# Cross-attention on one core: query banks as two tiles, the context's sums in steps, seeds moved, another order in the first rounds and the tail

## The chip, the core and the metric

The kernel runs on one core of a Trainium2 chip. A core has four compute engines that take their instructions each in its own order and wait for each other by semaphores: TensorE (PE, matrix products, with the loading of weights shown as PEld), VectorE (DVE), ScalarE (ACT) and GpSimd (POOL). SyncE (SP) issues the transfers between DRAM and the on-chip memory; SPq in a profile is its queue. Products land in PSUM, which the kernel uses in banks of 128 partitions x 512 float32. The metric is the time of one execution on the device, in microseconds. Two timed runs of the kernel before gave 1520.61 and 1522.45, a median of 1521.53.

## What is computed

For each of 64 batches, `H_l` is a 256 x 512 block of x and `H_a` a 256 x 384 block of the context, all float32:

```python
text_p = jnp.einsum('bld,dh->blh', H_l, W_text) + b_text
audio_p = jnp.einsum('bsd,dh->bsh', H_a, W_audio) + b_audio
Q = layer_norm(text_p, g1, beta1)
K = layer_norm(audio_p, g2, beta2)
V = audio_p
scores = jnp.einsum('blh,bsh->bls', Q, K) * scale
alpha = jax.nn.softmax(scores, axis=-1)
H_hyper = jnp.einsum('bls,bsh->blh', alpha, V)
H_hyper = jnp.einsum('blh,hk->blk', H_hyper, W_out) + b_out
return layer_norm(H_hyper + H_l, g_out, beta_out)
```

## The kernel before

All engines' instructions stand in an order written out by hand: each call in the main function emits instructions, and the engine takes them in the order of the calls. A program then adds the waits that the data need; it tracks them by tile.

**Two projections by fewer products.** The keys (`Thirds`, name k) and the output (`Thirds`, name y, called `o`) are computed in 15 products of 128 x 128 by 128 x 172 instead of 18, the queries (`Fork`) in 7 products of two halves each instead of 8, with sums formed beforehand and afterwards. Each product is two passes of PE and so two rows of a profile. `third_sides` (L298) has GpSimd form seven sums of the transposed context `cT` (tile csum) or of the transposed result `zT` of the attention (tile zsum); the products that need them are numbered. Product 14 and 13, the first two, need the fourth and fifth of these seven operations. `sum_x` (L282) has GpSimd form four sums of the transposed x (tile xsum).

**Stages of a projection.** `Thirds` keeps its partial results in the banks ps_m, ps_l, ps_u, ps_n, the same four for k and o, which take turns. `seed` (L504, ACT) writes a bias into ps_m; `one` writes ps_n, `two` adds to ps_m, `three` to ps_u, and so on to `five`; `after_one`, `after_three`, `after_four` (DVE) carry sums from bank to bank in between. `after_five` (L541, ACT and DVE), `leave` (ACT) and `last_middle` (L552, POOL operations d and kr) take k's result out of the banks; `leave_plus` (L558, DVE) takes o's out and adds x. It calls `between()` in its midst, which is DVE's reciprocal of the softmax sums (`reciprocals`, L682).

`Fork` has one PSUM tile ps_f of two banks (L66): R and q1 in the first, q2 and q3 in the second. `seed` (L583, ACT) writes the bias into R and zeros into q2, in one copy from a prepared tile fork_seed. `one` adds x's first quarter into R, `after_one` (L598, ACT) copies R to q1, `seven` adds into q2, `after_seven` (L601, ACT) copies q2 to s7, `six` adds into R, `after_six` (L608, DVE) writes q3 and steps R, `five` adds into R, `after_five` (DVE) writes q2, and `rest` finishes. `square`, `scales` (POOL: ve and rstd) and `normalise` (ACT) then make the rows of unit variance.

**A round** (L1045 to L1192) works on several batches at once: it projects keys and queries of batch b + 2 (k2, q2), transposes the inputs of b + 3 and forms their sums, turns the stored q and k of b + 1 (through DRAM and back: `store`, `fetch`, `turn` on DVE), takes scores and softmax of b (`at`), the attention's product of b - 1 (`last`, context_one) and b - 2 (`old`, context_two) and the output of `old`, and normalises the output of b - 3 (`settled`: `sums`, `deviations` on ACT with ve and rstd on POOL, `shift` L882 and `settle` L891 on DVE). PE's order in a round is k2.one, k2.two, context_two, k2.three, q2.seven, q2.six, k2.four, q2.five, k2.five, q2.rest, score, o.one, o.two, score, o.three, score, o.four, score, o.five, the next q's one, context_one. Softmax is `maxima` (DVE, nmx), `exponentials` (ACT, e), `reciprocals` (DVE, rden), `divide_e` (ACT); e is stored to DRAM, fetched and turned by DVE (`store_e`, `fetch_e`, `turn_e`, tile eT) for the next round's context_one.

In the steady rounds k2.seed stands behind divide_e (L1189), Fork.seed behind o.five (L1159), and sum_x and third_sides of b + 3 stand together near the round's end, x first (L1165 and L1166). Before the rounds (L925 to L1043) the first batches are projected, the weights of the output folded, and the weights' sums formed (`third_weights`, L324). After them (L1194 to L1293) the last batches are finished; there `transpose_e` (PE) and `copy_e` (ACT) take the place of the way through DRAM for the last two.

Of the kernel before, what the change touches and what calls it, by code (L numbers as in the profile page):

```python
# [22 lines left out]
def kernel(  # L23
# [41 lines left out]
    third = [p_all.tile([P, H], F32, tag=f"t{n}", name=f"ps_{n}") for n in "mlun"]  # L65
    fork = p_all.tile([P, 2, H], F32, tag="fork", name="ps_f")  # L66

# [109 lines left out]
    def keep_busy(n):  # L177

        for _ in range(n):
            nc.tensor.matmul(fork[:, 1, :P], lhsT=ones, rhs=ones, start=True, stop=True)  # L180

# [115 lines left out]

    def third_sides(T, tag, pool=work):  # L298

        a0, a1 = T[:, :, :P], T[:, :, P:]  # L300
        s = pool.tile([P, 10, P], F32, tag=tag, name=tag)
        plus = lambda o, i0, i1: nc.gpsimd.tensor_tensor(o, i0, i1, ALU.add)  # L302
        less = lambda o, i0, i1: nc.gpsimd.tensor_tensor(o, i0, i1, ALU.subtract)  # L303
        less(s[:, 0:2], a0[:, 0:1].broadcast_to([P, 2, P]), a0[:, 1:3])
        less(s[:, 2:4], s[:, 0:2], a1[:, 0:1].broadcast_to([P, 2, P]))
        plus(s[:, 4:6], s[:, 2:4], a1[:, 1:3])
        plus(s[:, 6], s[:, 4], a1[:, 2])
        plus(s[:, 7], s[:, 5], a1[:, 1])
        less(s[:, 8], s[:, 6], a0[:, 2])
        less(s[:, 9], a1[:, 0], a0[:, 0])  # L310
        return {
            14: s[:, 6], 13: s[:, 7], 11: s[:, 0], 12: s[:, 1], 9: s[:, 8], 8: s[:, 2],
            10: s[:, 3], 0: a0[:, 1], 3: a0[:, 2], 1: s[:, 9], 7: a1[:, 0], 2: a1[:, 1],
            4: a1[:, 2], 6: s[:, 4], 5: s[:, 5],
        }

# [55 lines left out]
    class Projection:  # L372
# [79 lines left out]
        def turn(self, halves=range(2)):  # L452
            if 0 in halves:
                self.T = work.tile(
                    [P, HC, self.nt * P], F32, tag=f"{self.name}T", name=f"{self.name}T_{self.b}"
                )
            if self.name == "q" or self.b >= B - 2:
                if 0 in halves:
                    turn(self.T, self.sq, HC)
                return  # L460

            for t in halves:
                nc.vector.transpose(
                    self.T.rearrange("p k (q t j) -> p t q k j", t=self.nt, j=SQ)[:, t],
                    self.sq[:, t * NQ : (t + 1) * NQ].rearrange("p q (k i) -> p q k i", k=HC),
                )
# [14 lines left out]
    class Thirds(Projection):  # L481
# [11 lines left out]
        def add_products(self, *pairs):  # L493
            for n, place in pairs:
                nc.tensor.matmul(  # L495
                    place,
                    lhsT=self.sides[n],
                    rhs=self.weights[n],
                    start=(n == 14),
                    stop=True,  # L500
                    skip_group_check=True,
                )
# [55 lines left out]
        def leave_plus(self, x, between):  # L558
            rows = self.rows
            u, n, v = self.room("u"), self.room("n", 2), self.room("d")  # L560
            dve(n, self.M, ends(x[:, 1]), ALU.add)
            dve(u, self.U, middle(x[:, 1]), ALU.add)
            dve(v, self.N0, u, ALU.add)
            dve(middle(rows[:, 1]), v, self.N1, ALU.subtract)
            dve(ends(rows[:, 1]), self.N, n, ALU.add)
            between()
            u = self.room("u")
            dve(u, self.U, middle(x[:, 0]), ALU.add)
            dve(middle(rows[:, 0]), self.T, u, ALU.add)
            dve(ends(rows[:, 0]), self.L, ends(x[:, 0]), ALU.add)  # L570

    class Fork(Projection):

        R, q1 = fork[:, 0, :H2], fork[:, 0, H2:]
        q2, q3 = fork[:, 1, :H2], fork[:, 1, H2:]

# [5 lines left out]
        @staticmethod  # L582
        def seed():  # L583
            nc.scalar.copy(fork[:, :, :H2], fork_seed)

# [37 lines left out]
        def square(self):  # L623
            self.var = small.tile([P, 2], F32, tag="varq", name="var")
            for t in range(2):
                junk = work.tile([P, H], F32, tag="junk", name="junk")
                nc.scalar.activation(  # L627
                    junk,
                    fork[:, t, :],
                    AF.Square,  # L630
                    scale=1.0 / math.sqrt(H),
                    accum_out=self.var[:, t : t + 1],
                )

        def normalise(self):
            for t in range(2):
                nc.scalar.mul(self.rows[:, t, :], fork[:, t, :], self.r[t])

    class Attention:
# [110 lines left out]
        def start_products(self):  # L750

            sides = third_sides(self.zT, "zsum", once)
            self.o = Thirds("y", self.b, sides, wao_blocks, bao_sb, bao_delta)
            self.y = self.o.rows
# [167 lines left out]
    q, k, xT, cT, xs, cs, att = {}, {}, {}, {}, {}, {}, {}  # L922
    bank = third + [fork[:, n, :] for n in range(2)]

# [49 lines left out]
    k[1].evict(1)  # L974
    fork_seed = const.tile([P, 2, H2], F32, tag="fork_seed", name="fork_seed")
    nc.vector.tensor_copy(fork_seed[:, 0], bt_sb[:, H2:])
    nc.vector.memset(fork_seed[:, 1], 0.0)
    bt_step = const.tile([P, H2], F32, tag="bt_step", name="bt_step")
# [30 lines left out]
    q[1].after_seven()  # L1009
    part = bias_parts()  # L1010
    fold_multiply(2, 0, 2)
    q[1].six()
# [8 lines left out]
    q[1].rest()  # L1021
    wa_t = const.tile([P, 11, W3], F32, tag="wa_thirds", name="wa_thirds")
    wa_blocks = third_weights(wa_sb, wa_t, [0])
    cT[2] = turn_c(2)
    cs[2] = third_sides(cT.pop(2), "csum")
    xT[2] = turn_x(2)
    third_weights(wa_sb, wa_t, [1], nc.vector)
    q[1].square()
    q[1].scales()
    xs[2] = sum_x(xT.pop(2))  # L1030
    ba_delta = third_bias(ba_sb, "ba_delta")
    bao_delta = third_bias(bao_sb, "bao_delta")
    q[1].normalise()
# [11 lines left out]
    for b in range(B - 2):  # L1045
# [18 lines left out]
        if b == 0:  # L1064
            at.score(0, 8)
            Fork.seed()
        k2 = k[b + 2] = Thirds("k", b + 2, cs.pop(b + 2), wa_blocks, ba_sb, ba_delta)
        if b == 0:
# [30 lines left out]
        if settled:  # L1099
            settled.deviations()  # L1100
        k2.four()
        k2.after_four()
# [11 lines left out]
        k2.leave()  # L1114
        k2.last_middle()
        if old:
            old.o.seed()
# [26 lines left out]
        if b:  # L1144
            at.score(4, 7)
        q2.normalise()
        q2.store()
# [15 lines left out]
        k2.fetch()  # L1163
        if three:
            xs[b + 3] = sum_x(xT.pop(b + 3))  # L1165
            cs[b + 3] = third_sides(cT.pop(b + 3), "csum")  # L1166
        if b < 2:
            wao_blocks = third_weights(wao_sb, wao_t, [b])
        at.maxima()
        at.exponentials()  # L1170
        if not three:
            att[b + 1] = Attention(b + 1)
            att[b + 1].affine_queries()
            att[b + 1].affine_keys()
        if last:
# [9 lines left out]
        if last:  # L1185
            last.context_one()
        at.divide_e()
        if three and old:
            k2.seed()  # L1189
        at.store_e()  # L1190
        if last:
# [3 lines left out]
    at = att[B - 2]  # L1195
    last.fetch_e()

    load_x_rows(B - 3)
# [4 lines left out]
    old.o.seed()  # L1203
    at.score(0, 8)
    settled.statistics()
    settled.shift(0)
    settled.shift(1)
    k[B - 1].turn()
    at.maxima()
    at.exponentials()  # L1210
    at.reciprocals()
    old.o.one()
    old.o.after_one()
    old.o.two()
    last.turn_e()
    last.context_one()
# [5 lines left out]
    last.copy_two()  # L1222
    q[B - 1].turn()
    k[B - 1].affine(g2_sb, be2_sb)
    at.transpose_e(bank[4])
    at.copy_e()
    old.o.four()
    old.o.after_four()
    settled.settle(0)
    settled.settle(1)  # L1230
    settled.store()
    last.start_products()
    q[B - 1].affine(g1_sb, be1_sb)
    end = Attention(B - 1)
    old.o.five()
    old.o.leave_plus(x_rows[B - 4], lambda: None)
# [4 lines left out]
    add_bias(B - 1)  # L1241
    end.score(0, 8)
    old.shift(0)
    old.shift(1)
    last.o.one()
    last.o.after_one()
    last.o.two()
    end.maxima()
    end.exponentials()
    end.reciprocals()  # L1250
    at.start_output()
    at.multiply(0, bank[5])
    last.o.three()
    last.o.after_three()
    at.multiply(1, bank[4])
    old.settle(0)
    old.settle(1)
    old.store()
    at.evict(0)
    at.scales(0, 1)  # L1260
    last.o.four()
    last.o.after_four()
    end.transpose_e(bank[5])
    end.copy_e()
    last.o.five()
    at.evict(1)
    at.scale_soon(1)
    last.o.leave_plus(x_rows[B - 3], lambda: None)
    end.context()
    last.statistics()  # L1270
    at.shift(0)
    at.settle(0)
    at.shift(1)
# [52 lines left out]
```

## Time and profile before

| | |
|---|---|
| median of two runs | 1521.53 us |
| the profiled execution | 1522.37 us |
| its span, first to last instruction | 1520.6 us |
| PE busy | 1414.6 us (93%), 7419 matmuls |
| DVE busy | 1184.7 us (78%) |
| ACT busy | 1116.4 us (73%) |
| POOL busy | 983.4 us (65%) |
| moved by DMA | 322.54 MB, 212 GB/s on average |
| mean granted clock of PE | 0.990 |

Durations are those of one execution. An engine's share of busy time is an average over the span; where an engine waits, the profile names who released it last. The start of the next instruction can lie before the recorded end of the one ahead, since both are pipelined: for a chain, distances of starts are added up, not durations. By stretches, PE was busy 21.53 of the 30 us from 30 to 60, 18.84 from 60 to 90 and 25.12 from 90 to 120, at clocks of 0.94, 0.83 and 0.94; 287.08 of the 300 from 1000 to 1300; and 49.45 of the last 71, from 1450 on.

### The profile page before, as it was taken

To read this page: it belongs to the slowest core of one execution; us is meant where nothing else is said; L and a number is where in the kernel's file an instruction comes from. 1 tells how busy PE (TensorE), PEld (TensorE's weight loads), DVE (VectorE), ACT (ScalarE), POOL (GpSimd) and SP (SyncE) were. 2 spreads that over 40 slices of the span, in tenths; PEclk is the share of its full clock that TensorE was granted. 3 is DMA by queue.
4 is the path that set the end of the run, shared out by engine and by line. 5 is a ranking of instruction groups with operands and counts; after the bars stand their busy time and mean duration, and the time that the engine had idled before them with its cause. 6 is when DMAs were issued, how large, how long until landed. Compare 5 with 4: busy or idle time off the path is not lost.

```text
span 1520.6 us, 26267 instructions
## 1 busy us (share of the span) xinstructions
PE 1414.6 (93%) x7419; PEld 1235.6 (81%) x7419; DVE 1184.7 (78%) x2501; ACT 1116.4 (73%) x2813; POOL 983.4 (65%) x1685
## 2 busy tenths in 40 slices
PE   9679999999999999999999999999999999999976
PEld 4468888888888888888888888888888888888864
DVE  6537788788887887887878878878888888787757
ACT  4447877777777777787787787787777777777753
POOL 4576666666666667667667666666666666666724
PEclk9989999999999999999999999999999999999999
DMA  9577889889999889889998988988998988998761
GB/s 214 123 186 192 208 221 235 212 215 238 211 224 232 215 220 230 219 213 227 228 212 220 234 209 220 236 212 212 241 209 222 235 213 220 232 217 212 209 187 70
DMA packets 450456, 322.54 MB, mean 212 GB/s; under 512 B 154885, under 2 KB 382981, under 8 KB 450310
## 3 DMA queue, kind: packets, MB, share of 16 engines
q1 hardware_dynamic: 450214, 320.72, 86.5%
q8 instruction: 60, 0.98, 0.3%
q14 instruction: 86, 0.70, 0.2%
q10 hardware_dynamic: 96, 0.13, 0.0%
HBM read 203.83 MB, written 116.92 MB: 211 GB/s over the span
## 4 chain that ended last, share of the span: by engine, by line
PE 50%; DVE 16%; ACT 12%; DMA 10%; issue 6%; SPq 5%; POOL 2%; DVEq 0%; ACTq 0%; POOLq 0%
PE ps_f L588 15%; PE ps_m L495 11%; PE ps_sc L657 8%; DMA xq<-in_x_dram 7%; PE ps_z L723 4%; PE ps_u L495 4%; SPq L72 4%; PE ps_n L495 4%; ACT e L688 4%; DVE yr L479 3%; ACT kT L470 3%; PE ps_l L495 2%; DVE nmx L667 2%; DVE n L479 2%; DMA ed<-e 1%
## 5 line engine op out<-in xcount | busy, mean ns | idle before, releaser
L657 PE MATMUL ps_sc<-kT,qT 128*128 128x256 f32 x1024 | 261.0, 379 | 2.8 <-ACT zT L738 2.8
L588 PE MATMUL ps_f<-wtsum,xsum 128*128 128x256 f32 x756 | 201.4, 389 | 41.2 <-ACT s L603 39.0
L657 PEld LDWEIGHTS ps_sc<-kT,qT 128*128 128x128 f32 x1024 | 186.4, 190 | 20.5 <-ACT zT L738 3.4
L588 PEld LDWEIGHTS ps_f<-wtsum,xsum 128*128 128x128 f32 x756 | 132.9, 190 | 79.2 <-ACT s L603 64.7
L723 PE MATMUL ps_z<-eT,c 128*128 128x256 f32 x768 | 189.8, 385 | 6.4 <-DVE eT L75 6.4
L303 POOL TENSOR_TENSOR zsum<-zT 128x256 f32<-128x256 f32 x124 | 73.7, 595 | 186.5 <-ACT zT L741 173.9
L723 PEld LDWEIGHTS ps_z<-eT,c 128*128 128x128 f32 x768 | 143.0, 193 | 26.6 <-DVE eT L75 7.3
L674 ACT ACTIVATE e<-ps_sc,nmx 128x256 f32<-128x256 f32 x128 | 59.5, 470 | 130.7 <-DVE nmx L667 130.7
L369 POOL TENSOR_TENSOR rstd<-ve,nhalf 128x2 f32<-128x2 f32 x192 | 136.1, 709 | 16.0
L470 ACT ACTIVATE kT<-kT,columns 128x256 f32<-128x256 f32 x256 | 139.6, 596 | 0.0
L470 ACT ACTIVATE qT<-qT,columns 128x256 f32<-128x256 f32 x256 | 138.7, 591 | 0.0
L479 DVE TENSOR_TENSOR ps_f<-ps_f,s 128x256 f32<-128x256 f32 x126 | 54.5, 432 | 107.1 <-PE ps_f L588 104.1
L588 PE MATMUL ps_f<-wt,xT 128*128 128x256 f32 x504 | 130.5, 382 | 0.0
L367 POOL TENSOR_SCALAR ve<-var 128x2 f32<-128x2 f32 x126 | 27.7, 220 | 142.8 <-ACT junk L627 129.9
L891 DVE SCALAR_TENSOR_TENSOR yr<-yr,rstd,beo 128x512 f32<-128x512 f32 x124 | 114.6, 926 | 0.9 <-POOL rstd L369 0.9
L688 ACT ACTIVATE e<-e,rden 128x256 f32<-128x256 f32 x124 | 56.2, 500 | 71.9 <-DVE rden L684 71.9
L302 POOL TENSOR_TENSOR zsum<-zsum,zT 128x256 f32<-128x256 f32 x186 | 99.9, 552 | 9.7
L302 POOL TENSOR_TENSOR csum<-csum,cT 128x256 f32<-128x256 f32 x186 | 99.1, 547 | 9.7
L303 POOL TENSOR_TENSOR csum<-cT 128x256 f32<-128x256 f32 x124 | 99.4, 801 | 6.9 <-DVE cT L75 6.9
L588 PEld LDWEIGHTS ps_f<-wt,xT 128*128 128x128 f32 x504 | 94.0, 192 | 10.3 <-issue 0.3
L532 DVE COPY t<-ps_u 128x172 f32<-128x172 f32 x124 | 41.8, 337 | 75.6 <-PE ps_u L495 75.6
L882 DVE SCALAR_TENSOR_TENSOR yr<-yr,nm,go 128x512 f32<-128x512 f32 x124 | 93.8, 758 | 7.3 <-ACT junk L775 7.3
(230 smaller groups left out, 3980.1 us busy)
## 6 DMA issues: line engine op xcount, KB each, us to landing
kd<-kr SPq DMA_DIRECT2D x64, 512.0 KB, 4.2
kq<-kd SPq DMA_DIRECT2D x256, 128.0 KB, 3.6
qd<-qr SPq DMA_DIRECT2D x64, 512.0 KB, 4.8
qq<-qd SPq DMA_DIRECT2D x256, 128.0 KB, 3.6
xq<-in_x_dram SPq DMA_DIRECT2D x252, 128.0 KB, 5.5
x<-in_x_dram SPq DMA_DIRECT2D x63, 512.0 KB, 4.3
out_dram<-yr SPq DMA_DIRECT2D x62, 512.0 KB, 3.1
cq<-in_ctx_dram SPq DMA_DIRECT2D x252, 96.0 KB, 5.9
```

Source lines behind the costliest of these rows:

```text
L302: plus = lambda o, i0, i1: nc.gpsimd.tensor_tensor(o, i0, i1, ALU.add)
L303: less = lambda o, i0, i1: nc.gpsimd.tensor_tensor(o, i0, i1, ALU.subtract)
L369: nc.gpsimd.tensor_tensor(r, ve, nhalf[:, :n], ALU.pow)
L470: nc.scalar.activation(self.T[:, k, :], self.T[:, k, :], AF.Identity, bias=bet[:, k : k + 1], scale=gam[:, k : k + 1],)
L479: nc.vector.tensor_tensor(o, i0, i1, op)
L495: nc.tensor.matmul(place, lhsT=self.sides[n], rhs=self.weights[n], start=(n == 14), stop=True, skip_group_check=True,)
L588: nc.tensor.matmul(place, lhsT=side, rhs=w, start=False, stop=True, skip_group_check=True)
L657: nc.tensor.matmul(self.sc[:, t, :], lhsT=self.qT[:, k, bass.ts(t, P)], rhs=self.kT[:, k, :], start=(k == 0), stop=(k == HC - 1),)
L688: nc.scalar.mul(self.e[:, t, :], self.e[:, t, :], self.rden[:, t : t + 1])
L723: nc.tensor.matmul(ps, lhsT=c_rows[self.b][:, s, bass.ts(j, P)], rhs=self.eT[:, s, :], start=(s == 0), stop=(s == ST - 1),)
L882: nc.vector.scalar_tensor_tensor(row, row, self.nm[:, t : t + 1], go_sb, ALU.add, ALU.mult)
L891: nc.vector.scalar_tensor_tensor(self.y[:, t, :], self.y[:, t, :], self.r[t], beo_sb, ALU.mult, ALU.add)
```

## The change

The two query banks become two tiles. `Fork.seed` writes only R, straight from the bias; a new `Fork.clear` has DVE zero q2, and stands behind `maxima`. `third_sides` becomes a class `Sides`, whose `add(n)` emits the next n of the same seven operations; those of b + 3 are emitted two behind q2.after_six, three behind k2.last_middle, two ahead of sum_x. `k2.seed` goes ahead of divide_e, `between()` ahead of two more steps of leave_plus. In the first rounds, weight sums, turns and sums of batch 2 go ahead of q[1].six. In the last round e is not stored; the tail transposes it on PE instead, and its other steps stand in a new order. The class `Sides` keeps the operations, their order and their operands.

```diff
-    fork = p_all.tile([P, 2, H], F32, tag="fork", name="ps_f")
+    fork = [p_all.tile([P, H], F32, tag=f"f{n}", name=f"ps_f{n}") for n in range(2)]
...
+        def add(self, n=7):
+            for step in self.steps[:n]:
+                nc.gpsimd.tensor_tensor(*step)
+            self.steps = self.steps[n:]
+            return self
...
-            if self.name == "q" or self.b >= B - 2:
+            if self.name == "q" or self.b >= B - 3:
...
             dve(v, self.N0, u, ALU.add)
+            between()
             dve(middle(rows[:, 1]), v, self.N1, ALU.subtract)
             dve(ends(rows[:, 1]), self.N, n, ALU.add)
-            between()
...
         def seed():
-            nc.scalar.copy(fork[:, :, :H2], fork_seed)
+            nc.scalar.copy(Fork.R, bt_sb[:, H2:])
+
+        @staticmethod
+        def clear():
+            nc.vector.memset(Fork.q2, 0.0)
...
     part = bias_parts()
+    wa_t = const.tile([P, 11, W3], F32, tag="wa_thirds", name="wa_thirds")
+    wa_blocks = third_weights(wa_sb, wa_t, [0])
+    third_weights(wa_sb, wa_t, [1], nc.vector)
+    cT[2] = turn_c(2)
+    cs[2] = Sides(cT.pop(2), "csum").add()
+    xT[2] = turn_x(2)
+    xs[2] = sum_x(xT.pop(2))
     fold_multiply(2, 0, 2)
     q[1].six()
...
         q2.after_six()
         if settled:
             settled.deviations()
+        if three:
+            cs[b + 3] = Sides(cT.pop(b + 3), "csum").add(2)
         k2.four()
...
         k2.last_middle()
+        if three:
+            cs[b + 3].add(3)
         if old:
             old.o.seed()
...
             at.score(4, 7)
+        if not three:
+            att[b + 1] = Attention(b + 1)
+            att[b + 1].affine_queries()
         q2.normalise()
...
         if three:
+            cs[b + 3].add()
             xs[b + 3] = sum_x(xT.pop(b + 3))
-            cs[b + 3] = third_sides(cT.pop(b + 3), "csum")
...
         at.maxima()
+        if three:
+            Fork.clear()
+        if not three:
+            att[b + 1].affine_keys()
         at.exponentials()
...
-        at.divide_e()
         if three and old:
             k2.seed()
-        at.store_e()
+        at.divide_e()
+        if three:
+            at.store_e()
...
-    last.fetch_e()
-
     load_x_rows(B - 3)
...
     at.score(0, 8)
+    last.transpose_e(bank[4])
     settled.statistics()
-    settled.shift(0)
-    settled.shift(1)
+    last.copy_e()
     k[B - 1].turn()
+    q[B - 1].turn()
     at.maxima()
...
-    end.score(0, 8)
-    old.shift(0)
-    old.shift(1)
     last.o.one()
     last.o.after_one()
     last.o.two()
-    end.maxima()
-    end.exponentials()
-    end.reciprocals()
     at.start_output()
     at.multiply(0, bank[5])
     last.o.three()
     last.o.after_three()
-    at.multiply(1, bank[4])
+    end.score(0, 8)
+    old.shift(0)
+    old.shift(1)
+    at.evict(0)
+    at.scales(0, 1)
...
```

## The prediction

> **What bounds the kernel now.** I first read the stretches of the steady part: TensorE (PE) is busy 287.10 of 300 us at a full clock of 1.00, VectorE (DVE) 244.00.
>
> ```profile
> 700.00:1000.00 300.00, 287.10 (x1545) 255.44 (x1545) 244.00 (x517) 231.15 (x585) 199.51 (x344) 1.00 0.91 222
> ```
>
> So PE sets the pace, with a few per cent of holes. Then the waits, for who makes the holes (total, times, longest):
>
> ```profile
> PE ps_f L588 <- ACT s L603: 39.0, 63, 4.5
> PEld ps_n L495 <- POOL csum L302: 33.3, 60, 9.8
> PE ps_m L495 <- ACT ps_m L505: 28.3, 59, 3.0
> ```
>
> About once in each of the 62 rounds of the loop. Then the timeline of one round, PE's rows first (start, duration, engine and line, operation, count; waits in brackets):
>
> ```profile
> 712.56 1.89 PE L723 MATMUL ps_z<-eT,c 128*128 128x256 f32 x8
> 714.44 0.82 PE L495 MATMUL ps_n<-wa,csum 128*128 128x172 f32 x4
> 715.70 0.85 PE L495 MATMUL ps_m<-wa,csum 128*128 128x172 f32 x4 [0.44 <-ACT ps_m L505]
> 716.39 1.03 PE L723 MATMUL ps_z<-eT,c 128*128 128x256 f32 x4
> 717.25 0.46 PE L495 MATMUL ps_u<-wa_thirds,csum 128*128 128x172 f32 x2
> 717.54 1.03 PE L588 MATMUL ps_f<-wtsum,xsum 128*128 128x256 f32 x4
> 719.12 1.13 PE L588 MATMUL ps_f<-wtsum,xsum 128*128 128x256 f32 x4 [0.55 <-ACT s L603]
> ```
>
> and DVE's of the same round:
>
> ```profile
> 710.05 1.09 DVE L891 SCALAR_TENSOR_TENSOR yr<-yr,rstd,beo 128x512 f32<-128x512 f32 x1
> 711.07 0.68 DVE L667 TENSOR_REDUCE nmx<-ps_sc 128x2 f32<-128x512 f32 x1
> 711.67 0.69 DVE L75 STREAM_TRANSPOSE eT<-eq 128x512 f32<-128x512 f32 x1
> ...
> 713.78 0.52 DVE L479 TENSOR_TENSOR yr<-ps_n,n 128x344 f32<-128x344 f32 x1
> 714.21 0.15 DVE L684 RECIPROCAL rden<-den 128x2 f32<-128x2 f32 x1
> ...
> 721.79 0.77 DVE L882 SCALAR_TENSOR_TENSOR yr<-yr,nm,go 128x512 f32<-128x512 f32 x1
> 722.61 0.43 DVE L479 TENSOR_TENSOR ps_f<-ps_f,s 128x256 f32<-128x256 f32 x1
> 722.96 0.74 DVE L882 SCALAR_TENSOR_TENSOR yr<-yr,nm,go 128x512 f32<-128x512 f32 x1
> 723.61 0.74 DVE L891 SCALAR_TENSOR_TENSOR yr<-yr,rstd,beo 128x512 f32<-128x512 f32 x1
> ```
>
> The reader is to see starts, not durations. eT recurs at 734.25: a round is 22.58 us. Undisturbed, groups of four matmuls follow each other every 0.86 us (256 wide) or 0.58 (172 wide). Three places are slower. k2.one (714.44) comes 0.15 after the eight of ps_z should end. k2.two (715.70) waits 0.68 for the seed of ps_m (715.22, 0.43 long) and restarts 0.11 slower. q2.six (719.12) comes 0.72 late for the copy s7 (718.72, 0.35 long), plus 0.11. Sum 1.77; a PE that never waits would need 20.8.
>
> **The steady rounds, part by part.** Times in a round count from k2.one (714.44; the one before 691.86).
>
> *Separate bank tiles.* In the built order q2.six no longer waits for after_seven, only for after_one, which ended at 713.18. All 0.83 goes; s7 stays ahead of its reader, after_six.
>
> *k2.seed ahead of divide_e.* It needs only the first step of leave_plus (ended 712.76) and ScalarE (ACT) free at 713.18, so it ends near 713.6; k2.two wants it at 714.9. The 0.79 goes with 1.2 of cover; each us beyond that would cost a us. Divide_e follows as soon as its reciprocal, now some 0.8 earlier in DVE's order, is there; its store ed is still issued behind kq (715.82 to 717.60, ed 717.70), so nothing on SyncE's queue (SP) moves. Seeding one bank instead of two saves ACT 0.23 (0.59 against the 0.36 of a 256-wide copy), worth nothing there: ACT waits 2.1 for nmx right after.
>
> *DVE from o.four to k2.one.* k2.one overwrites ps_n, which leave_plus reads last at 713.78 to 714.30, just when csum ends (714.29). So csum alone gains nothing. DVE takes 5.80 from o.four's ps_m matmuls (708.64) to k2.one, PE 5.63. Fork.clear puts a memset between nmx and eT: 0.27 by the one memset of this size (L977); below, 0.19, its distance to the next start; above, 0.43, DVE's add into ps_f; an added operation cannot gain. I take 0.27, the same operation. The reciprocal moves ahead of that read: 0.07 (714.21 to 714.28). Settle(1) (710.05) takes 1.09 instead of settle(0)'s 0.74 (723.61), beside GpSimd's sums of x; these now start later, and I give back 0.25 of the 0.35 (bounds 0 and 0.35). 5.89 remain: PE waits about 0.26.
>
> *What is late next: settle(0).* Unhindered, o.three would start at 14.90 - 1.62 = 13.28 (old: 706.76). It needs DVE's ps_u, and behind settle(0) DVE has kr, kr, qT, xT, n and ps_u: starts 0.66+0.35+0.45+1.17+1.12+0.37 apart, plus 0.39 to land: 4.51. Settle(0) (old: 9.17) waits for GpSimd (POOL): seven zsum steps (4.12) after the zT copy, then ve and rstd (722.70, 0.70 long). The zT copy starts at 2.47 instead of 3.01, since divide_e and the seed are out of its way; zsum then ends at 7.04 undisturbed. But shift(0) moves from 7.35 to about 5.9, into zsum. DVE operations with two SBUF inputs and POOL sums hold each other up: csum's first step took 1.18 beside settle(1), zsum's same step 0.73. Shift(0) and shift(1) each cost POOL some 0.4, so rstd ends at 8.9 to 9.2, no sooner than before (8.96). Behind rstd, POOL now issues csum's first two steps at once; at the tail, where POOL's L829 starts 0.08 before settle, the two settles took 2.40 instead of 1.5, so POOL goes first. Settle(1) at 710.05 lost 0.35 to a sum of x that ended at 710.59, so it was let go some 0.19 before that end; a csum step of 0.73 then holds settle(0) for about 0.5, and it starts at 9.4 to 9.7. o.three comes at 13.9 to 14.2, 0.6 to 0.9 late, plus 0.1 restart: I take 0.9. Ends: 0, if settle(0) is never late (less is not possible, PE goes in order); 1.9, if both csum steps go first (0.81 more) and the shifts cost another 0.2.
>
> The Trainium skill speaks against this placing: SBUF — State Buffer, "Who interferes with whom", says that a VectorE instruction with two SBUF inputs and a GpSimd instruction that reads SBUF exclude each other for the whole instruction. The row lets the waiting one go earlier than that; by the rule settle(0) would wait the whole step, 0.19 more, and the sum below would be 58 x 0.19 = 11 us higher.
>
> POOL's other csum steps (1.7 before ve of q) push that rstd to about 14.8, and the R seed to 16.5; q3.one wants it near 19.1 (3.06 after o.four's ps_m). Cover 2.6. The rest of csum and the sums of x end near 20, needed 2.3 into the next round.
>
> New round: 13.28 + 0.9 + 1.88 (o.three to o.four's ps_m) + 5.89 = 21.95, 0.63 less. Rounds 3 to 60 are of this kind: 58 x 0.63 = 37 us. With lateness 0: 21.05, 89 us. With 1.9, a memset of 0.43 and no relief at settle(1): 23.36, 45 us lost.
>
> **First rounds.** k2.one waited 9.37 us at 78.80 and 2.52 at 102.62 for csum, which POOL now sums while it idled (7.11 before d at 67.61). What is late next at b = 1 is after_one on ACT, behind kT's affine (ends 78.06): six moves from 85.75 to about 78, 8 us; at b = 2, 2.5, and 1 at two smaller waits. Ahead of them DVE's weight sums (4.6 us, L329 and L330) now stand before q[1].after_six and delay POOL's q scales by about 1, against 1.2 gained at six of b = 0. Together 11; ends 5 (ACT later) and 15.
>
> **Tail.** score waited 2.77 for zT behind eight affines of ACT; ps_z waited 4.80 for eT by way of DRAM and then ran its fours in 1.9 instead of 0.86. Affines move ahead; four transposes (0.60) and a copy (0.57) replace store and fetch. Against that, the last score moves behind more products, and what follows it to the end (29 us) stays as long. The one more kT that is turned in one operation (1.23 instead of 2 x 0.70) costs nothing. I take 7; ends 0 and 12.
>
> Sum: the profiled execution, 1522.37 (span 1520.6, 1.77 around it), less 37, 11 and 7 is 1467.4; the median shown is 0.84 lower: **1466.5 us**.
>
> **Rivals.** *All holes close*: settle(0) wins the port or starts early; POOL idled 2.1 before ve of q, which speaks for room, and rstd at 8.9 against it. Late by 0 to 0.4, a round is 21.05 to 21.45: with the ends' 18, 1415 to 1438. *Nothing but the ends*: the queue of transfers takes over. From qd's issue (708.22) to the end of xq's issues (729.26) are 21.04 us of issues and landings, 21.6 in another round; 7% longer landings and issues in a shorter round make 22.5; with the ends that is 1499, with poorer or better ones 1487 to 1516. An untouched wait at six would end here too; the built order speaks against it. *Slower*: DVE gets the port only when POOL's run ends. Shift(0) then waits 1.1 for zsum, settle(0) 1.3 for two csum steps: o.three another 1.7 late (2.4 less the 0.5 and some 0.2 already counted), a round 23.65, 58 x 1.07 - 18 = 44 us lost, 1566; it decides from rounds above 22.9, where the ends' 18 us are used up. Against it: shift(0) at 721.79, in the middle of a zsum step, took 0.77.
>
> **The numbers.** Forecast (rounds 21.45 to 22.3, 1438 to 1487) 0.55; all holes 0.17; ends only 0.19; slower 0.09. A fifth left out at both sides gives 1428 to 1510. About 2% (1491 to 1552) is what a measurement tells from no change: faster 0.55 + 0.17 + 0.04 = 0.76; same 0.15 + 0.02 = 0.17; slower 0.07.
>
> **What would show it.** Right: the waits of ps_f on s and of ps_m on its seed vanish; PE waits instead at o.three for DVE's ps_u (some 0.8 a round) and at k2.one for DVE (0.3); settle(0) takes about 1.2; a round 21.95. Wrong: settle(0) at 0.74 right behind rstd, or q3.one waiting for the seed of R, or eT, qT or kT waiting for a DMA.

## The result, and the profile after

The kernel after took 1469.46 us (two runs, 1468.37 and 1470.56), against 1521.53 before: a ratio of 0.966, 95% interval 0.9616 to 0.9699. The prediction was 1466.5. Its sum had three terms, and the starts of nmx, which occurs once in a block, give what each became (differences of starts, us):

| stretch of the profiled execution | before | after | gain | predicted |
|---|---|---|---|---|
| start to the fourth nmx | 146.8 | 131.9 | 14.8 | 11 |
| the next 58 rounds | 1309.6 | 1271.3 | 38.3 | 37 |
| the rest, to the end | 64.2 | 63.3 | 0.9 | 7 |

The middle line hides more than it shows. Before, all but three of the 58 rounds take 22.57 to 22.62. After, the mean is 21.92, 0.03 off the predicted 21.95, but no round is typical: 25 lie between 21.01 and 21.5, most of these at 21.33 to 21.35, and the others reach up to 25.01. So there is a floor of 21.33, and something else on top.

The stretches of after (stretch, its length, busy time of PE, PEld, DVE, ACT and POOL with their instructions, clock of PE, DMA share, GB/s), and then its waits (total, times, longest):

```profile
700.00:1000.00 300.00, 291.91 (x1595) 263.75 (x1594) 254.77 (x550) 233.69 (x603) 215.65 (x354) 1.00 0.90 231
```

```profile
PEld ps_u L502 <- POOL ve L374: 24.9, 54, 0.5
PEld ps_z L734 <- DVE yr L486: 22.0, 13, 2.1
PE ps_z L734 <- DMA c<-in_ctx_dram: 17.0, 19, 1.9
```

PE's waits of ps_f on s and of ps_m on its seed, 39.0 and 28.3 us before, are gone from the head of the list. New is a short wait at o.three (ps_u, 54 times 0.46). The row names GpSimd's ve, which writes nothing that this product reads; it is VectorE's write of ps_u: PE starts 0.49 behind the start of that write in all 52 such rounds between 200 and 1350, as it does in the tail, where the row names VectorE (1420.94 and 1421.43 below). New too is a wait of ps_z, the context product, for the rows of c. It appears in 19 rounds under DMA, and in others under a DVE instruction that had ended long before, but it is the same wait: in the ten late rounds whose landing of c the trace has, ps_z starts 0.14 behind the landing, whichever engine is named. Here is one such round on the timeline (start, duration; waits in brackets), PE's rows first, then the queue of SP:

```profile
762.42 1.03 PE L668 MATMUL ps_sc<-kT,qT 128*128 128x256 f32 x4
763.53 0.53 PE L502 MATMUL ps_u<-wao_thirds,zsum 128*128 128x172 f32 x2
...
771.03 1.97 PE L734 MATMUL ps_z<-eT,c 128*128 128x256 f32 x8 [1.46 <-DMA c<-in_ctx_dram]
```

```profile
764.19 0.42 SPq L100 DMA_DIRECT2D c<-in_ctx_dram  x1
764.67 1.94 SPq L72 DMA_DIRECT2D cq<-in_ctx_dram  x4
766.65 4.57 SPq L72 DMA_DIRECT2D xq<-in_x_dram  x4
771.40 0.38 SPq L448 DMA_DIRECT2D qd<-qr  x1
```

ps_u starts 1.11 behind the group of ps_sc instead of 0.86: that is o.three, 0.25 late. ps_z starts 6.84 behind the issue of c. Before, it started 9.7 to 11.4 behind it in the steady rounds, so landings of about 6 us never showed; now the distance is 5.0 to 7.5, and the landing decides. xq's four issues take 4.57 and qd follows at once: the queue has no slack left there.

At settle(0) the row is as the prediction had it. GpSimd ends rstd and goes on to csum; VectorE, which waited for rstd, starts 0.07 behind and takes 1.21 instead of the 0.74 of settle(1). These are VectorE's row and then GpSimd's of one round:

```profile
452.73 1.21 DVE L902 SCALAR_TENSOR_TENSOR yr<-yr,rstd,beo 128x512 f32<-128x512 f32 x1 [0.87 <-POOL rstd L376]
```

```profile
452.00 0.70 POOL L376 TENSOR_TENSOR rstd<-ve,nhalf 128x2 f32<-128x2 f32 x1
452.66 0.73 POOL L320 TENSOR_TENSOR csum<-cT 128x256 f32<-128x256 f32 x1
```

In the tail the old holes of 2.77 and 4.80 are gone, but there is one of 3.04 at 1443.87, and a new one stands at o.three (PE's rows, then VectorE's):

```profile
1413.98 1.89 PE L734 MATMUL ps_z<-eT,c 128*128 128x256 f32 x8
1421.43 0.91 PE L502 MATMUL ps_u<-wao_thirds,zsum 128*128 128x172 f32 x2 [5.56 <-DVE ps_u L486]
```

```profile
1416.47 1.25 DVE L75 STREAM_TRANSPOSE kT<-kq 128x1024 f32<-128x1024 f32 x1 [7.17 <-DMA kq<-kd]
1417.64 1.20 DVE L75 STREAM_TRANSPOSE qT<-qq 128x1024 f32<-128x1024 f32 x1
...
1420.94 0.34 DVE L486 TENSOR_TENSOR ps_u<-ps_n,n 128x172 f32<-128x172 f32 x1
```

zsum, the product's other operand, had ended on GpSimd at 1413.23. What PE waits for, old.o.after_one, stands on VectorE behind two transposes, and the first of these waits 7.17 us for a transfer. That one stood ahead of after_one before, too, behind two shifts:

```profile
1468.76 1.25 DVE L75 STREAM_TRANSPOSE kT<-kq 128x1024 f32<-128x1024 f32 x1 [1.21 <-DMA kq<-kd]
```

Counted from the nmx of the 62nd block, it started at 12.4 us before and at 13.2 after. The transfer is hardly later, but PE, without its old holes, now comes to o.three ahead of it; the second transpose, 1.20 long, is what the change put in between.

### The profile page after: what moved, and what is told of

It is laid out like the page before. It is cut to its first block, busy times and chain, and to the rows that moved or that the text cites. A ratio compares the mean times of both kernels' runs of the same rounds, so it can differ in the third digit from the quotient of the medians.

```text
span 1466.6 us, 26207 instructions
## 1 busy us (share of the span) xinstructions
PE 1398.7 (95%) x7423; PEld 1240.0 (85%) x7423; DVE 1201.9 (82%) x2560; ACT 1096.4 (75%) x2814; POOL 1022.0 (70%) x1685
## 2 busy tenths in 40 slices
DMA packets 449094, 322.00 MB, mean 220 GB/s; under 512 B 153781, under 2 KB 381621, under 8 KB 448950
## 4 chain that ended last, share of the span: by engine, by line
PE 36%; DMA 31%; POOL 12%; DVE 10%; SPq 5%; issue 4%; ACT 2%; DVEq 0%; POOLq 0%; ACTq 0%
DMA kd<-kr 11%; PE ps_f L599 9%; PE ps_m L502 6%; POOL csum L320 5%; PE ps_z L734 5%; DMA cq<-in_ctx_dram 5%; DMA kq<-kd 5%; PE ps_sc L668 5%; PE ps_u L502 4%; SPq L72 4%; DMA c<-in_ctx_dram 4%; PE ps_n L502 3%; DMA qd<-qr 3%; PE ps_l L502 2%; DMA qq<-qd 2%
## 5 line engine op out<-in xcount | busy, mean ns | idle before, releaser
L320 POOL TENSOR_TENSOR zsum<-zsum,zT 128x256 f32<-128x256 f32 x310 | 196.2, 650 | 14.6
L320 POOL TENSOR_TENSOR csum<-csum,cT 128x256 f32<-128x256 f32 x310 | 192.0, 628 | 9.8
L599 PE MATMUL ps_f<-wtsum,xsum 128*128 128x256 f32 x756 | 186.3, 383 | 4.8 <-ACT ps_f L610 4.1
L902 DVE SCALAR_TENSOR_TENSOR yr<-yr,rstd,beo 128x512 f32<-128x512 f32 x124 | 120.7, 975 | 52.1 <-POOL rstd L376 52.1
L599 PEld LDWEIGHTS ps_f<-wtsum,xsum 128*128 128x128 f32 x756 | 139.6, 192 | 21.0 <-ACT ps_f L610 4.9
L893 DVE SCALAR_TENSOR_TENSOR yr<-yr,nm,go 128x512 f32<-128x512 f32 x124 | 102.7, 830 | 0.4 <-ACT junk L786 0.4
L486 DVE TENSOR_TENSOR ps_l<-ps_m,t 128x172 f32<-128x172 f32 x248 | 85.7, 346 | 17.0
L557 ACT COPY kr<-ps_l 128x344 f32<-128x344 f32 x62 | 27.6, 446 | 86.5 <-DVE kr L486 86.2
L786 ACT ACTIVATE junk<-yr,nm 128x512 f32<-128x512 f32 x124 | 87.9, 712 | 0.0
L438 ACT ACTIVATE kr<-kr,rstd 128x512 f32<-128x512 f32 x126 | 84.0, 720 | 3.7 <-POOL rstd L376 3.7
```

The source lines that it names most:

```text
L320: nc.gpsimd.tensor_tensor(*step)
L438: nc.scalar.mul(row, row, self.r[t])
L486: nc.vector.tensor_tensor(o, i0, i1, op)
L599: nc.tensor.matmul(place, lhsT=side, rhs=w, start=False, stop=True, skip_group_check=True)
L786: nc.scalar.activation(junk, self.y[:, t, :], AF.Square, bias=self.nm[:, t : t + 1], accum_out=self.ssq[:, t : t + 1],)
L893: nc.vector.scalar_tensor_tensor(row, row, self.nm[:, t : t + 1], go_sb, ALU.add, ALU.mult)
```

## The experiments

All ratios are to the kernel before, timed beside it on the same chip. It took 1524.18 beside e1 to e4, 1521.12 beside e5 to e8 and 1522.00 beside e9 to e12, so across these groups the ratios compare better than the medians. "Round" is the distance of the starts of nmx, the median of the 58; the kernels compute the same and differ in the order of instructions, in e1 and e2 also in the query banks and their seeds.

| run | median us | ratio, 95% interval | round |
|---|---|---|---|
| e1 bank split alone, on before | 1489.49 | 0.9775 (0.9759 to 0.9791) | 22.17 |
| e2 after, one bank tile | 1473.26 | 0.9663 (0.9642 to 0.9685) | 21.66 |
| e3 after, store of the softmax rows e ahead | 1432.44 | 0.9401 (0.9383 to 0.9418) | 21.33 |
| e4 after, rows of c first | 1433.56 | 0.9408 (0.9394 to 0.9422) | 21.33 |
| e5 e3, csum's first steps later | 1424.97 | 0.9365 (0.9347 to 0.9384) | 21.15 |
| e6 e3, memset later | 1422.81 | 0.9352 (0.9338 to 0.9366) | 21.16 |
| e7 e3, seed behind divide_e | 1433.16 | 0.9419 (0.9404 to 0.9434) | 21.34 |
| e8 e3, turns of the tail later | 1429.33 | 0.9396 (0.9382 to 0.9410) | 21.34 |
| e9 e3, csum whole | 1448.22 | 0.9517 (0.9501 to 0.9532) | 21.51 |
| e10 e3, seed and reciprocal back | 1476.29 | 0.9692 (0.9678 to 0.9707) | 22.05 |
| e11 e3 with e5, e6, e8 and one more | 1402.38 | 0.9210 (0.9197 to 0.9224) | 20.87 |
| e12 e3, first rounds as before | 1435.39 | 0.9427 (0.9413 to 0.9441) | 21.35 |

**e1: the bank split alone.** The kernel before with the tiles of the change:

```diff
-    fork = p_all.tile([P, 2, H], F32, tag="fork", name="ps_f")
+    fork = [p_all.tile([P, H], F32, tag=f"f{n}", name=f"ps_f{n}") for n in range(2)]
...
-            nc.scalar.copy(fork[:, :, :H2], fork_seed)
+            nc.scalar.copy(Fork.R, bt_sb[:, H2:])
...
         at.maxima()
+        if three:
+            Fork.clear()
...
```

> The kernel before with one part of the change: the two query banks are tiles of their own, R is seeded by ScalarE and q2 cleared by a memset on VectorE between nmx and eT; csum, the seed of ps_m, the first rounds and the tail stay as before. Theory of the prediction: the wait of ps_f on s goes (0.83 a round), k2.two still waits for its seed behind divide_e, and the memset (0.27) comes onto VectorE's path to k2.one, where nothing is relieved since the sums of x start where they did: a round of 22.58 - 0.83 + 0.27 = 22.0, so about 1522 - 60 x 0.56 = 1488 us, a ratio of 0.978. Rival: the wait at six was only the last of several, and the next one (the add of s by VectorE, or the seed) takes its place: a round of 22.4 or more, 1512 or more, no change.

1489.49: the prediction's theory. The wait at six is gone and 0.42 a round remains of its 0.83. Behind the memset, eT is now late for ps_z by 0.26, and k2.one is 0.29 late instead of 0.15, 0.1 of it because ps_z restarts slower; these take the rest.

**e2: the kernel after with one bank tile.** The same lines, the other way round.

> The kernel after with the two query banks in one tile again, seeded by one ScalarE copy, no memset; all else as after. The wait at q2.six should be back (0.83 a round). Theory A: the kernel after has rounds of 21.34 that TensorE and its short waits set, and longer ones where the loop of transfers on SyncE's queue is late; a wait of 0.83 less the memset's part (0.1 to 0.2) makes the rigid round 22.0 to 22.1, above most of the loop's, so that both do not add up: a round of about 22.1, 1474 to 1484 us, a ratio to the kernel before of 0.972. Theory B: lateness of transfers is added to whatever TensorE does: 21.92 + 0.7 = 22.6 a round, about 1508 us, 0.991.

1473.26, theory A. The floor of the rounds is 21.66, lower than expected, because PE waits at six and nowhere else: o.three (705.65), ps_z and k2.one (713.18) follow undisturbed. PE's rows in e2:

```profile
704.79 1.03 PE L664 MATMUL ps_sc<-kT,qT 128*128 128x256 f32 x4
705.65 0.46 PE L502 MATMUL ps_u<-wao_thirds,zsum 128*128 128x172 f32 x2
...
711.45 1.90 PE L730 MATMUL ps_z<-eT,c 128*128 128x256 f32 x8
713.18 0.75 PE L502 MATMUL ps_n<-wa,csum 128*128 128x172 f32 x4
...
717.08 1.13 PE L595 MATMUL ps_f<-wtsum,xsum 128*128 128x256 f32 x4 [0.55 <-ACT s L610]
```

So of the 0.83, 0.5 a round comes back as o.three's and k2.one's new waits, and since only five of the 58 rounds are longer than 22, the mean of e2, 21.77, is even below the 21.92 of after. Over the whole kernel the split earns nothing clear here: the ratio is 0.9663 in e2 and 0.9658 in after. What the trace shows for it lies at the start, where e2's fourth nmx comes at 145.1, 13.2 later than in after.

**e3: the store of e ahead of the fetches of q and k.**

```diff
-        q2.fetch()
-        k2.fetch()
         if three:
             cs[b + 3].add()
...
             at.store_e()
+        q2.fetch()
+        k2.fetch()
```

> The kernel after with the store of e (ed) issued ahead of the fetches of q and k (qq, kq) on SyncE's queue, by moving the fetches to the end of the round's body; so the 3.3 us in which ed lands pass while the queue waits for qd. Theory A (the queue's own order, with its waits for landings in a row, makes rounds longer than 21.34): waits of ps_z for the rows of c go, nearly all rounds take 21.34, 58 x 0.55 = 32 us less: 1434 to 1442. Theory B (the transfers' rate is the limit; DMA engines are busy 0.92 of the time): no change, 1464 to 1472.

**e4: the rows of c ahead of the fetch of e.**

```diff
+        if b > 1:
+            load_c_rows(b - 1)
         if last:
             last.fetch_e()
         if b > 1:
             load_x_rows(b - 1)
-            load_c_rows(b - 1)
```

> The kernel after with the rows of c issued ahead of the fetch of e and of the rows of x on SyncE's queue, some 2.3 us earlier. Theory A (the loop of the queue has a mean of 21.9 us whatever stands first in it): ps_z no longer waits for c, but another transfer (eq, kq, qq) becomes the late one; less than 8 us gained, 1460 to 1469. Theory B (only the lead of c is short): the waits go and nothing follows, rounds of 21.34 to 21.4, 1434 to 1442.

1432.44 and 1433.56. e3 came out by its theory A, e4 by its theory B: my view that the queue has a mean of its own, whatever stands first in it, fell. In both, all but two of the 58 rounds take 21.32 to 21.35, and in the steady rounds ps_z starts 11.0 to 12.8 us (e3) and 12.2 to 16.0 us (e4) behind the issue of c. This is SP's queue in after, and then in e3:

```profile
709.90 2.57 SPq L72 DMA_DIRECT2D qq<-qd  x4
...
714.71 0.40 SPq L703 DMA_DIRECT2D ed<-e  x1
718.00 1.78 SPq L72 DMA_DIRECT2D eq<-ed  x4
```

```profile
708.28 0.40 SPq L912 DMA_DIRECT2D out_dram<-yr  x1
708.78 0.41 SPq L448 DMA_DIRECT2D kd<-kr  x1
711.82 0.36 SPq L703 DMA_DIRECT2D ed<-e  x1
712.27 1.94 SPq L72 DMA_DIRECT2D qq<-qd  x4
...
720.32 0.40 SPq L100 DMA_DIRECT2D c<-in_ctx_dram  x1
```

In e3 the queue stood waiting for settle(1)'s rows (708.28) and for e (711.82), that is for the engines. In after it stood twice for a landing: for qd, from 706.56 to 709.90, and for ed, from 715.11 to 718.00. e4 puts the issue of c into the second stretch. e3 issues ed in the first, so that ed lands while qq and kq are issued, and eq follows kq at once (717.48): the second stretch is gone. Both edits shorten the queue's loop and lengthen the lead of c at once; which of the two it was, these runs do not tell apart. The transfers' rate was not the limit: the same 322.00 MB go through in a span of 1429.7 us in e3 and of 1466.6 in after.

**e5: csum's first two steps away from settle(0).** All five stand behind last_middle:

```diff
-        if three:
-            cs[b + 3] = Sides(cT.pop(b + 3), "csum").add(2)
...
-            cs[b + 3].add(3)
+            cs[b + 3] = Sides(cT.pop(b + 3), "csum").add(5)
```

> The kernel of e3_e_store_ahead (after, with the store of e ahead of the fetches; rounds of 21.34), and GpSimd's first two steps of csum moved behind k2.last_middle, so that all five stand together there and none runs beside settle(0). Theory A (the port: settle(0) takes 1.21 instead of 0.74 because csum's step of 0.73 starts 0.07 before it, and this is what makes o.three late by 0.25 + 0.08): settle(0) takes 0.74, o.three waits no more, a round of 21.0: 1432 - 60 x 0.33 = 1412 us, ratio 0.927. Theory B (settle(0) is long for another reason, or kr and what follows waits for GpSimd anyway): 1428 to 1436, 0.94.

1424.97, between the two. The mechanism is theory A's: settle(0) takes 0.75 and o.three follows at 0.86. VectorE's row in e5, then PE's:

```profile
718.47 0.75 DVE L902 SCALAR_TENSOR_TENSOR yr<-yr,rstd,beo 128x512 f32<-128x512 f32 x1 [0.87 <-POOL rstd L376]
```

```profile
701.11 1.03 PE L668 MATMUL ps_sc<-kT,qT 128*128 128x256 f32 x4
701.97 0.46 PE L502 MATMUL ps_u<-wao_thirds,zsum 128*128 128x172 f32 x2
...
707.77 1.93 PE L734 MATMUL ps_z<-eT,c 128*128 128x256 f32 x8
709.74 0.82 PE L502 MATMUL ps_n<-wa,csum 128*128 128x172 f32 x4
```

But of the 0.33 only 0.18 stays: k2.one is now 0.24 late instead of 0.10. PE became faster up to o.four, VectorE's path behind it did not, and settle(1) takes 0.88 there instead of 0.74 since the sums of x start earlier. The first rounds also lose 2.8 us.

**e6: the memset off VectorE's path to k2.one.**

```diff
         at.maxima()
-        if three:
-            Fork.clear()
...
         k2.after_one()
+        if b:
+            Fork.clear()
         k2.two()
```

> The kernel of e3_e_store_ahead with the memset of q2 moved on VectorE from between nmx and eT to behind k2.after_one (ahead of the transpose of cT). Theory A (the prediction's step: VectorE's path from o.four to k2.one is the longer one, and the memset is part of it): k2.one starts 0.10 earlier and its restart of 0.07 goes, a round of 21.17: 1432 - 60 x 0.17 = 1422 us, 0.933. Theory B (k2.one is late for eT or ScalarE, or the memset delays after_three by its 0.19 in the new place): 1430 to 1435.

1422.81 and a round of 21.16, where theory A had 1422 and 21.17. The price of the memset on this path is 0.18 to 0.19, its distance to the next start, not its recorded 0.27.

**e7 and e10: what the seed's place is worth.** e7 puts k2.seed behind divide_e again; e10 does so too and moves the reciprocal back as well:

```diff
-        if three and old:
-            k2.seed()
         at.divide_e()
+        if three and old:
+            k2.seed()
...
             dve(v, self.N0, u, ALU.add)
-            between()
             dve(middle(rows[:, 1]), v, self.N1, ALU.subtract)
             dve(ends(rows[:, 1]), self.N, n, ALU.add)
+            between()
```

> The kernel of e3_e_store_ahead with k2.seed behind divide_e again, as it was before the change. The prediction's step gives the 0.79 at k2.two to this move. If so, a round of 21.9 to 22.1 and 1465 to 1480 us. Rival, from the trace after: divide_e runs from 710.89 because the reciprocal stands earlier on VectorE (710.70), so a seed behind it would still end near 712.2, ahead of k2.two at 712.50; then the earlier reciprocal alone carries the gain: a round of 21.3 to 21.4, 1430 to 1437 us.

> The kernel of e3_e_store_ahead with both undone: k2.seed behind divide_e, and the reciprocal of den behind VectorE's reads of ps_n. e7 showed that the seed's place alone is worth nothing. Theory: either of the two is enough, since the seed waits for divide_e and divide_e for the reciprocal; with both back the seed ends near 713.1 of the shown round instead of 710.95 or 712.2, k2.two waits 0.5 to 0.7 and restarts 0.11 slower: a round of 21.95 to 22.1, 1468 to 1480 us. Rival: the wait at k2.two went through something else (csum, the bank split): 21.34, 1432.

e7: 21.34, nothing lost. e10: 22.05, and 1476.29. ScalarE's rows of e7, and then of e10 with PE's k2.two:

```profile
709.78 0.91 ACT L699 ACTIVATE e<-e,rden 128x256 f32<-128x256 f32 x2 [0.31 <-DVE rden L695]
710.59 0.44 ACT L512 COPY ps_m<-ba 128x344 f32<-128x344 f32 x1
```

```profile
707.92 0.91 ACT L699 ACTIVATE e<-e,rden 128x256 f32<-128x256 f32 x2 [1.23 <-DVE rden L695]
708.73 0.43 ACT L512 COPY ps_m<-ba 128x344 f32<-128x344 f32 x1
```

```profile
709.22 0.85 PE L502 MATMUL ps_m<-wa,csum 128*128 128x172 f32 x4 [0.44 <-ACT ps_m L512]
```

The seed ends at 711.03 in e7, 0.36 ahead of k2.two at 711.39. In e10 divide_e waits 0.92 longer for the reciprocal and the seed ends when k2.two has already waited. Either move alone closes the hole; the change made both.

**e8: the tail's turns.**

```diff
-    k[B - 1].turn()
-    q[B - 1].turn()
     at.maxima()
...
     old.o.after_four()
+    k[B - 1].turn()
+    q[B - 1].turn()
     settled.settle(1)
...
-    k[B - 1].affine(g2_sb, be2_sb)
     last.start_products()
...
+    k[B - 1].affine(g2_sb, be2_sb)
     q[B - 1].affine(g1_sb, be1_sb)
```

> The kernel of e3_e_store_ahead with the tail's turns of the last k and q moved on VectorE from ahead of at.maxima to behind old.o.after_four (and the affine of kT beside that of qT). Theory A (the hole of 5.56 us at o.three of the tail is VectorE's queue: after_one stands behind two transposes that wait for their transfers): the hole closes, 3 to 6 us less, 1427 (1426 to 1429). Theory B (the next wait, for the score of the last block or for VectorE at four, takes it back): 1431 to 1434.

1429.33, with an interval that overlaps e3's. The hole (3.86 in e3) closed as theory A had it: o.three follows at once and the nmx of the next block comes 4.5 earlier, but then PE's rows read

```profile
1391.73 0.82 PE L502 MATMUL ps_n<-wao,zsum 128*128 128x172 f32 x4 [1.68 <-DVE yr L486]
...
1404.96 1.51 PE L502 MATMUL ps_m<-wao_thirds,zT 128*128 128x172 f32 x4 [3.46 <-DVE ps_u L486]
1406.27 0.78 PE L502 MATMUL ps_u<-wao_thirds,zT 128*128 128x172 f32 x2
1406.84 4.49 PE L803 MATMUL ps_f<-wao,zT 128*128 128x512 f32 x6
```

The second hole (3.05 in e3, after_four behind shifts and settles on VectorE) is longer, and behind it the six products of ps_f take 4.49 at a clock of 0.61, instead of 2.74. The clock also blurs the gain. From the 62nd nmx to the end, e8 takes 58.7; the same code without its edit takes 59.8 in e3, where the clock stayed at 1.00 behind this hole, and 62.6 and 62.2 in e4 and e7, where it fell to 0.50 and 0.54 for 3 us, as it did in e8 (0.50). Against those two, alike in this, 3.5 to 3.8 us are gained; against e3, 1.1.

**e9: csum whole, behind the sums of x.**

```diff
-            cs[b + 3] = Sides(cT.pop(b + 3), "csum").add(2)
...
-            cs[b + 3].add(3)
...
-            cs[b + 3].add()
             xs[b + 3] = sum_x(xT.pop(b + 3))
+            cs[b + 3] = Sides(cT.pop(b + 3), "csum").add()
```

> The kernel of e3_e_store_ahead with csum summed whole behind the sums of x again, as before the change. The prediction's step (csum in steps gains nothing of its own: k2.one also waits for VectorE's last read of ps_n): k2.one comes some 0.4 later, since GpSimd ends csum's fifth step 4.0 behind o.four's ps_m instead of 3.57, but settle(0) gets the port at once and o.three's 0.33 goes: a round of 21.4 to 21.8, 1436 to 1460 us. Rival (csum in steps is what the gain at k2.one hangs on): the whole 4.1 us of csum stand behind the sums of x and k2.one comes 1.5 to 2 later, a round of 22.8 or more, 1520.

1448.22, as the prediction's step had it: settle(0) gets the port at once (0.75), o.three is on time, k2.one comes 4.03 behind the start of ps_m in o.five (which the expectation calls o.four's) instead of 3.57, and the round is 21.51. In the steady rounds csum in steps is worth 0.18: without it settle(1) stands beside a sum of x and takes 1.21, ps_z is 0.27 late for eT and k2.one 0.29 instead of 0.10, while o.three's 0.33 is won back. Another 5.8 us lie ahead of the fourth nmx, where k2.one waits 8.78 and 2.23 us for csum again.

**e12: the order of the first rounds.** third_weights, the turns of block 2, its csum and its sums of x stand behind q[1].rest() again.

> The kernel of e3_e_store_ahead with the order of the first rounds as before (sums of the weights, cT, csum, xT and the sums of x of block 2 behind q[1].rest). The prediction put 11 us (5 to 15) on this: 1443 us. The starts of nmx in the traces show 14.8 less up to the fourth round, of which the first three rounds' own gain of some 1.2 each is not this order's: 11 again. Rival (csum in steps and the banks give most of it): under 6 us, 1438 or less.

1435.39 and 2.3 more than e3 at the fourth nmx, which comes at 130.9 to 132.2 in e3, e7, e8 and e10, all with the new order: the rival. The 9.37 us of k2.one at 78.80 did not come back with this order; it came back with e9. The expectation misread the prediction here: its 11 us rest on k2.one's waits for csum, which GpSimd now sums in steps around d, so on csum in steps and not on this order.

**e11: a faster kernel.** e3 with the edits of e5, e6 and e8, and in the tail

```diff
-    old.settle(0)
-    old.settle(1)
-    old.store()
     last.o.four()
     end.maxima()
     last.o.after_four()
     end.exponentials()
     end.reciprocals()
+    old.settle(0)
+    old.settle(1)
+    old.store()
```

> The kernel of e3_e_store_ahead with e5's move of csum's first steps, e6's move of the memset, e8's move of the turns in the tail, and in the tail the two settles of block B-4 behind last.o.after_four and the end's reciprocals. If o.three's 0.33 and k2.one's 0.17 to 0.24 both go, a round is 20.84 to 20.95: 60 x 0.45 = 27 us; the tail 1 to 4: 1400 to 1405 us, ratio 0.92. Rival: one takes the other's gain back (settle(1) beside the sums of x, as in e5): 21.1, 1415.

1402.38, 0.921 of before, and so 0.954 of after (0.9210 over 0.9658). The round of 20.87 is within 0.1 of the 20.8 that the prediction gave for a PE that never waits; together the two edits give 0.46 where alone they gave 0.18 and 0.17. PE is now busy for 98% of the span:

```profile
PE 1369.9 (98%) x7423; PEld 1241.2 (89%) x7423; DVE 1175.2 (84%) x2560; ACT 1099.1 (78%) x2814; POOL 1039.4 (74%) x1685
```

## Why the prediction held, and where it did not

The time is right to 3 us, but that close only by luck: two errors of 0.6 us a round cancel, and at the two ends 4 us too little stand against 6 too much.

*The bank split removes 0.83*: right as to the wait. The hole at six is gone in after and in e1, and is back in e2; e1 keeps 0.42 of it.

*k2.seed ahead of divide_e removes 0.79*: the hole went, the cause was named too narrowly. With the reciprocal earlier the seed could have stayed (e7); only both undone bring 0.72 back (e10). The prediction noted that divide_e runs some 0.8 earlier and did not ask whether that was enough by itself.

*csum in steps alone gains nothing*: nearly right, 0.18 a round together with its cost at settle(0) (e9).

*k2.one waits 0.26*: 0.17 (0.10 and a restart of 0.07). The memset on that path is 0.18 to 0.19 (e6), the lower bound and not 0.27, and settle(1) is relieved of its whole 0.35 (0.74 in after) and not of 0.25.

*o.three 0.6 to 0.9 late, 0.9 taken with the restart*: the mechanism is right (e5), the size was not: 0.25 and 0.08. Settle(0) was let go 0.47 late as foreseen, but rstd ended 8.71 behind k2.one (720.56 and 711.85 in e3) and not at 8.9 to 9.2: of the two shifts only one held zsum up (its five middle steps take 3.35 instead of the 2.90 that they take in the tail), and the prediction charged 0.4 for each; the copy of zT also starts at 2.30 (714.15) and not at 2.47. This is the term that was mis-sized most.

On the 20.8 of a PE that never waits, these two waits make 20.8 + 0.17 + 0.33 = 21.3, the floor of 21.33; the prediction had 21.95.

*The queue of transfers* has no term in the sum: since ed is still issued behind kq, the prediction said, nothing on SP's queue moves. The order indeed did not move, but the rounds became shorter. As a rival the queue stood at a round of about 22.5, and it came in by half: on average 0.59 a round above the floor, spread over 33 of the 58. The transfer that PE waits for, c, was not among the three that the prediction named as a sign of being wrong (eT, qT, kT). The prediction counted SP's loop at 21.04 to 21.6 in the profile before: a floor of 21.33 meets that, one of 21.95 would not have. e2 shows the same from the other side: at a floor of 21.66 only a few rounds are late. The forecast of 21.95 is thus 0.62 too much for PE and VectorE, and 0.59 too little for the transfers.

*First rounds, 11*: 14.8, and not from where the prediction had it. It rested 10.5 on k2.one's two waits for csum; these went, but csum in steps is worth 5.8 (e9), since PE then waits 4.47 at 74.05 for VectorE's ps_u, where the prediction saw ScalarE's after_one as the next late one. The order of these rounds is worth 2.3 (e12). The bank split, which the prediction gave 1.2 at six of the first round, is worth 8.5 alone (e1) and up to 13.2 when taken from the rest (e2); these overlap and do not add up. Part of the 13.2 is the clock: in e2 it is 0.52 from 58 to 66, where the groups of four matmuls behind the two waits of ps_f at 60.73 and 63.30 take 2.05 and 2.08, and 0.50 from 82 to 90. Before, the same two waits, 0.59 and 0.52 long, left these groups at 1.10 and 1.13 and the clock at 1.00, so this is no fixed price of the waits; half the clock over these 16 us is some 8 us by estimate, and how much of that belongs to the split is open.

*Tail, 7*: 0.9. The step that failed: the prediction took the two old holes for gained and did not ask what is late next on VectorE. Its paragraph has no term for the turns of the last k and q: what "costs nothing" is the kT of an earlier batch. But the turn of the last k waits for kq, which lands no earlier than before, q's turn now stands there too, and after_one comes behind both. Taking that hole away gains 1 to 4 us (e8), since the next ones follow; how much of the 7 the tail could give is open. e11's tail is 57.2 against e8's 58.7, with one edit more, which was not tried alone.

*The lock of the port*, that is, the exclusion of GpSimd's sums and VectorE's operations with two inputs in SBUF. Settle(0) started 0.07 behind a step of 0.73 and took 0.47 longer, so it was let go some 0.19 ahead of the step's recorded end, the value taken from settle(1) before. The Trainium skill, SBUF — State Buffer, "Who interferes with whom", calls this an exclusive lock, held for the whole instruction, which would be 0.66; the measurement decides. That the two exclude each other, and that the first to start goes first, the rows and e5 agree with.

## What to carry to other kernels

Where several engines share a round, a hole that is closed is paid back at the next late place: ask for each removed wait what the floor becomes, and then compare that floor with the queue's own loop, since a rate that never showed at 22.6 can decide at 21.3. An early start on a queue that otherwise stands waiting for a landing is cheap: moving one issue in SP's queue gave 37 us, where the whole change had given 52. And when holes are closed or steps moved, look in each queue for the instruction that waits for a transfer; what stands behind it waits too.

## What the runs showed of the chip that was not expected

A pause of PE of 2 to 3 us can halve its clock for the next few us, and its length alone does not say whether it will. Stretches of after, behind pauses of 1.92 (at 419.23), 1.46 (at 771.03) and 5.56 (at 1421.43):

```profile
419.00:423.00 4.00, 3.77 (x11) 3.13 (x12) 0.93 (x3) 0.39 (x1) 0.00 (x0) 0.58 1.20 239
...
771.00:775.00 4.00, 3.97 (x21) 3.69 (x22) 2.54 (x7) 2.00 (x6) 0.00 (x0) 1.00 1.09 284
```

```profile
1421.00:1424.00 3.00, 2.57 (x7) 2.13 (x8) 2.93 (x7) 0.00 (x0) 0.00 (x0) 0.50 0.02 5
```

The third number from the right, ahead of the DMA share, is the granted clock. At 419.23 the eight of ps_z took 3.35 instead of 1.97, and that round is the longest of all, 25.01. Yet a pause of 2.77 before (at 1463.37) cost nothing: its sixteen took 3.72, no more than elsewhere at full clock (3.62 to 3.72), while one of 2.77 at the same place in e1 (at 1430.73) was followed by a clock of 0.65 over 3 us. Over all fourteen traces, no pause of 1.3 to 1.86 lowered the clock of the next 3 us, every one of 3.37 or more did, and of the 24 from 1.92 to 3.06 it was 16. The Trainium skill, TensorE: Matmul & The Clock Gate, "Part 1: The HAM clock gate", says that the gate looks at windows of about 3.4 us that run free of the program; a pause shorter than that would then count or not by where it falls, which fits these rows, but no run here set where a pause falls. Under "Why this matters for your kernels" it advises to avoid pauses of more than about 3 us; here 1.92 was enough once.
